# Group statistics on TensorE, the layer-2 residual on VectorE, and a new order of the third stage, in a four-layer convolution kernel

## The chip, the cores and the metric

The kernel runs on one core of a Trainium2 chip. The metric is the device time of one execution, in microseconds, taken as the median of several runs. Unless marked ns, all times below are microseconds.

## The reference

The input x is an image batch of shape (8192, 8, 16, 16): 8192 samples, 8 channels, 16 rows, 16 columns. Four layers follow, each of the form "normalize, transform, add to the input":

```python
x = x + L0(gn(x))     # a tensor-train operator over (8, 16, 16), plus bias
x = x + L1(gn(x))     # 3x3 convolution, batch norm over the whole batch, relu
x = x + L2(gn(x))     # 3x3 convolution on numbers rounded to int8 range, scale from max|gn(x)|
x = x + L3(gn(x))     # 3x3 convolution with weights sign(w) * mean|w|, edge padding

def gn(v, G=4, eps=1e-5):          # per sample and group of two channels: 512 numbers
    m, s = mean(g), var(g)         # over 2 channels, 16 rows, 16 columns
    return (g - m) / sqrt(s + eps)
```

Two sums go over everything and so cut the kernel into stages: the batch norm of layer 1 needs statistics of all samples, and the scale of layer 2 needs the largest absolute value of all normalized samples.

## The kernel before

**Tiling.** The batch is cut into NT = 64 tiles of 128 samples. A tile is held as [128 partitions, 2048]: the partition is (channel, row), 128 in all, and along the free axis stand 128 samples of 16 columns each. One tile is 1 MB. A group of the normalization is 32 partitions times the 16 numbers of a sample, so its sums need an addition across partitions and one across the 16 columns, and its results have to be spread back over the 32 partitions.

**Stages.** Stage 1 (to about 2640) computes layer 0 and the convolution of layer 1, and writes x and y of most tiles to memory. Stage 2 (lines 746 to 865; about 2640 to 3063) loads them, applies batch norm and relu (`sum2`), takes the group statistics, subtracts the mean (`centre2`), finds the largest normalized value (`range2`), and stores the centred tile, except for 13 tiles that stay on the chip. Stage 3 (lines 880 to 1053; 3063 to the end) rounds and convolves for layer 2, adds, takes new group statistics, convolves for layer 3, adds, and stores.

**Group statistics before.** `sums_pe` (line 708) multiplies the tile, and then its square, by `wsum`, a [128, 32] matrix that adds each group's 32 partitions. It is called on four quarters of 512 columns, each of which fills 32 rows of PSUM (32 samples of 16 columns), so that the four quarters stand in the four column groups of the TensorE array:

```python
for k, src in ((0, x), (1, sq)):
    for q in range(NQ):
        pe.matmul(ps[32 * q:32 * q + 32], L["wsum"][:, k], src[:, q * BANK:(q + 1) * BANK], ...)
```

VectorE then adds over the 16 columns (`tensor_reduce` in `stats_small`, line 719, and `stats2`, line 781) and transposes blocks of 32 by 32, so that samples stand on partitions and the four groups along the free axis; variance and `pow` (on GpSimd, line 729) follow on [128, 4]. To come back, `to_rows` (line 732) writes the four numbers of each sample through a mask into a [128, 4, 32] block diagonal, transposes that on VectorE, and TensorE multiplies the result by a selection matrix (`sel0`, `sel1`, `corr`), which gives a [128 partitions, 128 samples] array in PSUM. VectorE reads that array with each value repeated over the 16 columns (`over_w`).

**The steps of stage 3, for one tile.** The names are those of the dictionary `OPS` (line 1032) and are used in what follows:

- `rows2`, `spread2`: 1/sigma of stage 2, times the scale, spread over partitions (PSUM `ps_a`).
- `v` (line 925, VectorE): x times that, written as int8. `q` (933, ScalarE): v as bf16.
- `c2h0`, `c2h1` (942, TensorE): layer 2, six bf16 products for each half of the tile, into PSUM tiles `pq` of a pool `ps_c` with two buffers.
- `bias` (938, ScalarE) and `stz` (951, VectorE): bias and residual of the first half. `z1` (955, ScalarE) and `add1` (958, GpSimd): those of the second half.
- `sq`, `sums` (962, 965): the square on ScalarE and `sums_pe`; `small` (969, VectorE), `pow` (973, GpSimd): the statistics.
- `rows3`, `spread3`: three sets of rows, two products (`ps_r`, `ps_o`).
- `t` (982, VectorE): x/sigma. `hi` (993, ScalarE): t rounded to float32r, and its edge columns copied (`edges`). `lo` (998, GpSimd): t minus hi; `edl` (1011, ScalarE): its edges. Both hi and lo have two buffers (pool `wk3`).
- `c`, `corr` (976, 1003): the part of layer 3 that comes from mean and bias, evaluated on ScalarE and added by GpSimd; for the last three tiles VectorE does it.
- `c3h0`, `c3h1` (1014, TensorE): layer 3, twelve float32r products for each half (six of hi, six of lo), into `pf`, from the same pool as `pq`. `out0`, `out1` (1025, VectorE): scale and residual; the second of them issues the store.

**What sets the order.** All engine calls go through `InOrder` (line 33), which keeps them in the order in which the program makes them. Each engine works its own list from the front; the framework puts in the waits for data and for buffers. So an order written in the program is the order on each engine. In stage 2 that is the loop at lines 852 to 865. In stage 3 it is the list `todo` (line 1044): a turn `TURN`, in which each step stands with an offset in tiles, repeated; its first 151 and last 130 entries are replaced by the lists `C_HEAD` and `C_TAIL`, written out by hand. Loads of stage 3 (`load3`, line 896) are issued on the SP queue with `rows2`, four tiles ahead; x tiles have 13 slots, and the stores to the result stand on the same queue.

In the trace all recorded engine calls have line 43, so groups are told apart by tile names: `pf` (layer 3), `pq` (layer 2), `s` and `gs` (sums in stage 3 and 2), `ps_a`, `ps_r`, `ps_o`, `gb`, `gr` (spreads).

Of the kernel before, what the change touches and what calls it, by code (L numbers as in the profile page):

```python
# [18 lines left out]
P = 128  # L19
# [28 lines left out]
C_HEAD = """  # L48
rows2:0 spread2:0 v:0 rows2:1 q:0 spread2:1 c2h1:0 rows2:2 bias:0 v:1 spread2:2 rows2:3 c2h0:0 v:2 z1:0 q:1
spread2:3 stz:0 add1:0 bias:1 c2h1:1 sq:0 c2h0:1 z1:1 v:3 sums:0 stz:1 small:0 q:2 add1:1 c2h0:2 c2h1:2 bias:2  # L50
rows2:4 pow:0 sq:1 rows2:5 rows3:0 z1:2 spread2:4 spread3:0 stz:2 t:0 q:3 sums:1 hi:0 c:0 small:1 v:4 add1:2 pow:1
bias:3 c2h0:3 spread2:5 rows3:1 sq:2 c2h1:3 spread3:1 stz:3 lo:0 sums:2 t:1 rows2:6 corr:0 edl:0 small:2 c:1 q:4
z1:3 hi:1 c3h0:0 pow:2 c3h1:0 v:5 add1:3 rows3:2 out0:0 bias:4 out1:0 lo:1 sq:3 q:5 spread3:2 spread2:6 c2h0:4 c:2
corr:1 edl:1 c2h1:4 rows2:7 z1:4 stz:4 t:2 hi:2 sums:3 c3h1:1 small:3 v:6 c3h0:1 out1:1 c2h1:5 pow:3 bias:5 rows3:3
spread3:3 lo:2 out0:1 q:6 spread2:7 rows2:8 z1:5 edl:2 v:7 c:3 add1:4 sq:4 c2h0:5 c3h0:2 bias:6 t:3 corr:2 stz:5
sums:4 c3h1:2 small:4 add1:5 hi:3 out0:2 c2h0:6 pow:4 rows3:4 sq:5 out1:2 spread2:8 stz:6 spread3:4 t:4 lo:3 c2h1:6
z1:6 corr:3 edl:3 sums:5 c:4 hi:4 small:5 pow:5 bias:7 v:8 q:7 add1:6
""".split()
C_TAIL = """
c2h1:-4 sq:-5 rows2:-2 rows3:-6 out1:-8 spread3:-6 rows2:-1 spread2:-2 c2h0:-4 v:-2 sums:-5 stz:-4 z1:-4 q:-3 t:-6  # L60
edl:-7 c3h0:-7 q:-2 small:-5 c2h1:-3 c:-6 out0:-7 c2h0:-2 hi:-6 add1:-4 sq:-4 pow:-5 rows3:-5 z1:-3 spread3:-5
bias:-2 t:-5 stz:-2 lo:-6 edl:-6 sums:-4 small:-4 bias:-3 corr:-6 c:-5 spread2:-1 c2h0:-3 stz:-3 pow:-4 c3h1:-7
hi:-5 out1:-7 c3h0:-6 rows3:-4 spread3:-4 add1:-3 c2h1:-2 sq:-3 lo:-5 z1:-2 out0:-6 v:-1 c3h1:-6 edl:-5 q:-1 add1:-2
sums:-3 t:-4 corr:-5 c:-4 c3h1:-5 out1:-6 small:-3 sq:-2 pow:-3 hi:-4 out1:-5 lo:-4 rows3:-3 bias:-1 sums:-2 c2h1:-1
small:-2 z1:-1 spread3:-3 edl:-4 c2h0:-1 c3h0:-5 c:-3 t:-3 stz:-1 add1:-1 pow:-2 corr:-3 rows3:-2 c3h1:-4 hi:-3
spread3:-2 sq:-1 out0:-5 c:-2 corr:-4 sums:-1 t:-2 lo:-3 hi:-2 small:-1 pow:-1 out1:-4 c3h0:-4 corr:-2 rows3:-1
out0:-4 edl:-3 c3h0:-3 spread3:-1 t:-1 lo:-2 c3h1:-3 out0:-3 edl:-2 out1:-3 hi:-1 c:-1 lo:-1 c3h0:-2 c3h1:-2 edl:-1
out0:-2 c3h0:-1 out1:-2 corr:-1 c3h1:-1 out0:-1 out1:-1
""".split()

# [8 lines left out]
def tile_net(ctx: ExitStack, tc: tile.TileContext, xb, xt_in, pack0, pack1, pack2, out):  # L79
# [84 lines left out]
    def late_constants(late):  # L164
# [99 lines left out]
        mod32 = const.tile([P, 32], F32, name="mod32")  # L264
# [5 lines left out]
        for k, name in enumerate(("sel0", "sel1", "corr")):  # L270

            t = L[name] = const.tile([P, CH], F32, name=name)
            dve.tensor_copy(t.rearrange("p (g n) -> p g n", g=G),
                            mod32[:, G * k:G * k + G].unsqueeze(2).to_broadcast([P, G, CH // G]))
        yield "statistics"

    def diagonal(n):
        ts = []
        for k in range(2):
            t = const.tile([P, NQ, 32], F32, name=f"diag_{n}_{k}")  # L280
            nc.gpsimd.memset(t, 0.0)
            ts.append(t)
        return ts
# [424 lines left out]
    def sums_pe(ps, x, sq):  # L708

        for k, src in ((0, x), (1, sq)):  # L710
            for q in range(NQ):
                pe.matmul(ps[32 * q:32 * q + 32], L["wsum"][:, k], src[:, q * BANK:(q + 1) * BANK],
                          start=(k == 0), stop=(k == 1))


    def put_quarter(ps):
        nc.vector.tensor_copy(ps[:, 0:NQ], L["quarter"])

    def stats_small(mv, st, ps, name):

        s = small.tile([P, 32], F32, name=f"s_{name}", tag="s")
        dve.tensor_reduce(s, samples(ps), AX.X, ALU.add)
        dve.transpose(st, s)
        sq = small.tile([P, G], F32, name=f"sq_{name}", tag="sqm")
        dve.tensor_copy(mv[:, 0:G], st[:, 0:G])
        dve.tensor_tensor(sq, st[:, 0:G], mv[:, 0:G], ALU.mult)
        dve.scalar_tensor_tensor(mv[:, G:2 * G], st[:, G:2 * G], EPS, sq, ALU.add, ALU.subtract)

    def stats_pow(mv):
        pool.tensor_tensor(mv[:, G:2 * G], mv[:, G:2 * G], mhalf[:, :G], ALU.pow)  # L730

    def to_rows(diag, mask, cols, name):

        at = 0
        for c in cols:
            n = c.shape[1]
            dve.tensor_tensor(diag[:, :, at:at + n], c.unsqueeze(1).to_broadcast([P, NQ, n]),
                              mask.unsqueeze(2).to_broadcast([P, NQ, n]), ALU.mult)
            at += n
        rows = small.tile([P, P], F32, name=f"rows_{name}", tag="rows")  # L740
        dve.transpose(rows, diag.rearrange("p q j -> p (q j)"))
        return rows

# [5 lines left out]
    with tc.tile_pool(name="p2", bufs=2) as p2, tc.tile_pool(name="ps2", bufs=2, space=PSUM) as ps2:  # L749
# [3 lines left out]
        diag = diagonal("b")  # L753
        psc, mask2 = (ps2.tile([P, 96], F32, name=n, tag=n, bufs=1) for n in ("psc2", "mask2"))
        put_quarter(mask2)
        mask2 = mask2[:, 0:NQ]

# [7 lines left out]
        nc.vector.tensor_tensor(L["corr"], L["corr"], ksum, ALU.subtract)  # L765

# [10 lines left out]
        def sums2(i):  # L777
            T[i]["ps"] = ps2.tile([P, BANK], F32, name=f"gs_{i}", tag="gs")
            sums_pe(T[i]["ps"], T[i]["x"], T[i].pop("sq"))

        def stats2(i):

            st, mv = psc[:, 32 + 32 * (i % 2):64 + 32 * (i % 2)], gnst[:, order2[i]]
            red = small.tile([P, 32], F32, name=f"s_c{i}", tag="s")
            dve.tensor_reduce(red, samples(T[i].pop("ps")), AX.X, ALU.add)
            dve.transpose(st, red)
            T[i]["sq"] = small.tile([P, G], F32, name=f"sq_c{i}", tag="sqm")
            act.copy(mv[:, 0:G], st[:, 0:G])
            act.activation(T[i]["sq"], st[:, 0:G], AF.Square)

        def sigma2(i):
            st, mv = psc[:, 32 + 32 * (i % 2):64 + 32 * (i % 2)], gnst[:, order2[i]]
            dve.scalar_tensor_tensor(mv[:, G:2 * G], st[:, G:2 * G], EPS, T[i].pop("sq"), ALU.add, ALU.subtract)
            stats_pow(mv)

        def spread2(i):
            T[i]["gb"] = ps = ps2.tile([P, BANK], F32, name=f"gb_{i}", tag="gb")
            rows = to_rows(diag[i % 2], mask2, [gnst[:, order2[i]]], f"c{i}")
# [5 lines left out]
            for dst, sel in ((ps[:, 0:P], L["sel0"]), (T[i]["gr"][:, i % 4], L["sel1"])):  # L804
                pe.matmul(dst, sel, rows, start=True, stop=True)

        def centre2(i):
            x, ps = T[i]["x"], T[i]["gb"]
            engines = [dve, dve]
            if NT - 4 <= i < NT - 1:  # L810
                engines, mean = [dve, pool], small.tile([P, P], F32, name=f"gm_{i}", tag="rows")
# [33 lines left out]
        for i in range(NT + 4):  # L845
# [9 lines left out]
            on(i - 2, sums2)  # L855
            on(i - 3, spread2)
            on(i - 1, square2)
# [22 lines left out]
    with ExitStack() as s:  # L880
        wk = s.enter_context(tc.tile_pool(name="wk3", bufs=2))
# [7 lines left out]
        diag2, diag3 = diagonal("d"), diagonal("e")  # L889

        ps_a, ps_r, ps_o = (ps_s.tile([P, BANK], F32, name=f"ps_{n}", tag=n) for n in ("a", "r", "o"))
        r2, r3, o3 = ps_a[:, 0:P], ps_r[:, 0:P], ps_o[:, 0:P]
        put_quarter(ps_a[:, P:2 * P])
        mask, st3 = ps_a[:, P:P + NQ], ps_a[:, P + 32:P + 64]

# [11 lines left out]
        def rows2(i):  # L907
            T[i]["rows2"] = to_rows(diag2[i % 2], mask, [gnst[:, order[i], G:2 * G]], f"d{i}")

        def rows3(i):  # L910
            mv = T[i].pop("mv")
            mr = small.tile([P, G], F32, name=f"mr_{i}", tag="mr")
            dve.tensor_tensor(mr, st3[:, 0:G], mv[:, G:2 * G], ALU.mult)
            T[i]["rows3"] = to_rows(diag3[i % 2], mask, [mr, mv[:, G:2 * G], gnst[:, order[i], 0:G]], f"e{i}")


        def spread2(i):
            pe.matmul(r2, L["sel0"], T[i].pop("rows2"), start=True, stop=True)

        def spread3(i):  # L920
            rows = T[i].pop("rows3")
            pe.matmul(r3, L["sel1"], rows, start=True, stop=True)
            pe.matmul(o3, L["corr"], rows, start=True, stop=True)
# [14 lines left out]
        def bias2(i):  # L938
            x = halves(T[i]["x"])[:, 0]
            act.activation(x, x, AF.Identity, bias=L["bias2"], scale=1.0)  # L940

# [9 lines left out]
        def first2(i):  # L951
            x = halves(T[i]["x"])[:, 0]
            dve.scalar_tensor_tensor(x, T[i].pop(("pq", 0)), inv, x, ALU.mult, ALU.add)

        def second2(i):
            act.activation(z3[i % 2], T[i].pop(("pq", 1)), AF.Identity, bias=L["bias2"], scale=inv)

        def add2(i):
# [3 lines left out]
        def square3(i):  # L962
            act.activation(sq3, T[i]["x"], AF.Square)
# [159 lines left out]
```

## Time and profile before

| what | value |
|---|---|
| median of 3 runs | 3832.61 (3832.19 to 3832.81) |
| span of the profiled execution | 3831.5 |
| PE busy | 3606.5 (94%), 16326 instructions |
| DVE busy | 3406.9 (89%), 6319 |
| ACT busy | 2513.1 (66%), 2673 |
| POOL busy | 3040.9 (79%), 3101 |
| DMA | 960.93 MB, mean 251 GB/s |
| span 2640 to 3063 (stage 2): PE, DVE, ACT, POOL busy | 248.7, 392.4, 247.8, 347.4 of 422.9; DMA share 0.94 |
| span 3063 to 3831 (stage 3): PE, DVE, ACT, POOL busy | 747.0, 697.0, 577.0, 711.0 of 768.6; DMA share 0.41 |

PE is TensorE, PEld its weight loads, DVE VectorE, ACT ScalarE, POOL GpSimd, SP the engine whose queue issues most DMAs. A line of the timeline gives start, duration, engine, operation, output and inputs with shapes, and the number of instructions merged; in brackets stands the time for which the engine was idle before it, and what ended that. Durations of pipelined instructions overlap, so the distance from one start to the next is not the duration. A float32 product leaves two records in the trace, a float32r or bf16 product one.

### The profile page before, as it was taken

How to read it: one execution, taken by the hardware profiler on the slowest of the kernel's cores; microseconds unless marked ns; L12 is line 12 of the kernel's file. 1: busy time of each engine (PE TensorE's matmuls, PEld its weight loads, DVE VectorE, ACT ScalarE, POOL GpSimd, SP SyncE). 2: the span in 40 equal slices, each digit the busy share in tenths (PEclk: the TensorE clock that was granted, in tenths of full speed). 3: DMA queues.
4: the chain of work that ended last, by engine and by line, in shares of the span. 5: the costliest groups of instructions: out<-in, count | busy, mean ns of one | idle time of the engine just before them, and what ended most of it. 6: DMA issues, size and time to landing. Idle time of an engine off the chain costs nothing. (4 is left out here: it accounts for less than half of the span.)

```text
span 3831.5 us, 52833 instructions
## 1 busy us (share of the span) xinstructions
PE 3606.5 (94%) x16326; PEld 2127.6 (56%) x16326; DVE 3406.9 (89%) x6319; ACT 2513.1 (66%) x2673; POOL 3040.9 (79%) x3101
## 2 busy tenths in 40 slices
PE   8999999999999999999999999997655599999998
PEld 4666666666666666666666666662211155555555
DVE  8988888888888888888888888877998889999997
ACT  5666666666666666666666666665665477777775
POOL 4877778777777787777777877766887779999997
PEclk9999999999999999999999999998776699999999
DMA  5787787888877878788788788757999724444432
GB/s 212 255 268 258 258 266 251 270 253 262 270 256 258 267 250 271 253 262 267 258 261 266 250 271 252 258 187 281 422 425 425 301 110 176 187 185 178 185 145 99
DMA packets 210809, 960.93 MB, mean 251 GB/s; under 512 B 44896, under 2 KB 45152, under 8 KB 110048
## 3 DMA queue, kind: packets, MB, share of 16 engines
q1 hardware_dynamic: 173808, 692.22, 48.7%
q0 software_dynamic: 36288, 264.26, 23.4%
q8 instruction: 131, 2.15, 0.2%
q14 instruction: 150, 1.23, 0.1%
q10 hardware_dynamic: 432, 1.08, 0.1%
HBM read 578.84 MB, written 378.54 MB: 250 GB/s over the span
## 5 line engine op out<-in xcount | busy, mean ns | idle before, releaser
L43 PE MATMUL po<-u,core 128*128 128x512 f32 (+1 forms) x4112 | 1844.7, 591 | 0.0
L43 ACT COPY u<-pu 128x2048 f32<-128x2048 f32 x512 | 956.7, 1868 | 511.9 <-PE pu L43 511.8
L43 PEld LDWEIGHTS po<-u,core 128*128 128x128 f32 x4112 | 744.7, 190 | 737.1 <-issue 736.1
L43 PE MATMUL pu<-core2r,xl 128*128 128x256 f32 x4032 | 678.5, 310 | 4.5 <-ACT u L43 3.6
L43 PEld LDWEIGHTS pu<-core2r,xl 128*128 128x128 f32 x4032 | 527.9, 189 | 127.8 <-issue 123.0
L43 POOL TENSOR_TENSOR bs<-bs,xh 128x512 fp32r<-128x512 f32 (+1 forms) x253 | 325.6, 1287 | 201.0 <-ACT xh L43 200.9
L43 POOL TENSOR_TENSOR v<-e 128x128 f32<-128x128 f32 x750 | 397.9, 542 | 0.0
L43 DVE TENSOR_TENSOR xs<-po,xs 128x512 f32<-128x512 f32 x256 | 177.0, 692 | 217.5 <-PE po L43 217.5
L43 ACT ACTIVATE m<-pm,b 128x128 f32<-128x128 f32 x250 | 92.0, 368 | 395.5 <-PE pm L43 395.5
L43 PEld LDWEIGHTS pm<-v,fast 128*128 128x128 f32 x2000 | 262.5, 191 | 119.7 <-issue 106.2
L43 POOL TENSOR_TENSOR e<-x1n,x 128x512 f32<-128x512 f32 x250 | 306.2, 1225 | 23.9 <-ACT x L43 16.4
L43 DVE TENSOR_TENSOR bs<-bs,stat 128x1024 f32<-128x1024 f32 x252 | 290.8, 1217 | 2.1
L43 POOL TENSOR_TENSOR xs<-xs,w 128x2048 f32<-128x2048 f32 x64 | 291.5, 4554 | 0.6 <-DMA xs<-in_xt 0.6
L43 PE MATMUL pm<-v,fast 128*128 128x128 f32 x2000 | 263.6, 275 | 0.0
L43 ACT ACTIVATE x<-x1n 128x512 f32<-128x512 f32 x500 | 247.1, 545 | 7.6 <-DVE x1n L43 7.6
L43 POOL TENSOR_TENSOR mv<-mv,mhalf 128x4 f32<-128x4 f32 x127 | 130.8, 1030 | 138.1 <-DVE mv L43 138.1
L43 PE MATMUL pf<-hi,sign 128*128 128x512 f32 x768 | 227.7, 434 | 0.5 <-DVE xs L43 0.5
L43 POOL DMA_DIRECT2D xl<-limb_d x252 | 150.0, 595 | 96.9 <-ACT x L43 29.1
L43 PE MATMUL pf<-lo,sign 128*128 128x512 f32 x768 | 219.4, 423 | 0.0
L43 POOL TENSOR_TENSOR v<-r 128x128 f32<-128x128 f32 x500 | 215.9, 448 | 0.0
L43 ACT ACTIVATE sq<-xs 128x2048 f32<-128x2048 f32 x103 | 196.8, 1911 | 4.7 <-POOL xs L43 4.6
L43 PE MATMUL gb<-rows_c,sel 128*128 128x128 f32 x128 | 40.3, 409 | 167.3 <-DVE rows_c L43 167.3
(310 smaller groups left out, 7202.4 us busy)
## 6 DMA issues: line engine op xcount, KB each, us to landing
xl<-limb_d POOLq DMA_DIRECT2D x252, 1024.0 KB, 7.4
x_d<-xs SPq DMA_DIRECT2D x76, 1024.0 KB, 8.4
xs<-in_xt SPq DMA_DIRECT2D x64, 1024.0 KB, 7.5
bs<-in_xb SPq DMA_DIRECT2D x63, 1024.0 KB, 5.7
limb_d<-xh SPq DMA_DIRECT2D x1008, 64.0 KB, 4.3
limb_d<-bs SPq DMA_DIRECT2D x1008, 64.0 KB, 5.2
y_d<-ys SPq DMA_DIRECT2D x60, 1024.0 KB, 8.0
u<-x_d SPq DMA_DIRECT2D x34, 1024.0 KB, 5.9
```

Of the source, the lines that this page charges most:

```text
L43: return self.tc.keep_in_program_order(op(*args, **kwargs))
```

## The change

1. **Sums.** `sums_pe` no longer gives one product to a quarter of 512 columns, but one to each of the 16 image columns w: 128 samples, 16 elements apart in memory, added up in PSUM over w. Four column groups take w modulo 4. The result is [4 x 32, 128 samples], where before it was [4 x 32, 512].
2. **Transposes.** ScalarE copies that result to SBUF (`S`), and one product with it as the weights against eight columns of `mod32` (`fold`) adds the four column groups and puts samples on partitions. To come back in stage 2 and in `spread2` of stage 3, ScalarE widens each sample's numbers to 32 equal columns (`wide`) and a product with the identity transposes them. In stage 3 the three sets of rows stand in one [128, 128] tile `rows3[k]`; a product with the identity turns it (`rT`), ScalarE copies it (`rows`), and `r3` and `o3` spread it as before. Square of the mean is on ScalarE (`sq4`), variance and ratio on VectorE (`var`, `mr`).
3. **Layer 2's residual** is `stz0` and `stz1`, both on VectorE without bias. The bias goes into the square (`sq`), into the copied sums (`sbias`), into `t` (now a three-operand instruction) and into `c` (`bias23`). `bias`, `z1` and `add1` are gone.
4. **Order of stage 3.** `TURN`, `C_HEAD` and `C_TAIL` are replaced by a phase for each step and a period; step `op` of tile i stands at 10.78 i + phase. The special case of the last three tiles in `c` and `corr` is gone, the edges of hi are a step of their own (`edh`), and the second half of layer 3 stands ahead of the first. PSUM of stage 3 has a further bank (`ps_t`).

```diff
+PERIOD = 10.78
+PHASE = {"wide": 0, "spread2": 0.01, "v": 0.02, "q": 11, "c2h0": 13.3, "stz0": 18.2, "c2h1": 19.6, "stz1": 21.4, "sq": 25.8,
+         "sums": 31.9, "S": 33.2, "fold": 36.4, "sq4": 36.8, "var": 41.5, "pow": 48.2, "mr": 51.2, "m2": 53.8, "rT": 55.5,
+         "rows": 56.7, "r3": 59.8, "t": 61.9, "hi": 65.3, "o3": 67.3, "c": 68.6, "edh": 69.1, "lo": 73.4, "corr": 75.7,
+         "edl": 76.6, "c3h1": 84.2, "out1": 85.4, "c3h0": 86.3, "out0": 86.31}
...
     def sums_pe(ps, x, sq):
         for k, src in ((0, x), (1, sq)):
-            for q in range(NQ):
-                pe.matmul(ps[32 * q:32 * q + 32], L["wsum"][:, k], src[:, q * BANK:(q + 1) * BANK],
-                          start=(k == 0), stop=(k == 1))
+            for w in range(W):
+                rows = slice(32 * (w % 4), 32 * (w % 4) + 32)
+                pe.matmul(ps[rows], L["wsum"][:, k], samples(src)[:, :, w], start=(k == 0 and w < 4), stop=(k == 1 and w >= W - 4))
+    def fold_pe(st, rows):
+        pe.matmul(st, rows, L["mod32"][:, 0:2 * G], start=True, stop=True)
+    def wide(dst, src):
+        act.copy(dst.rearrange("p (g n) -> p g n", n=CH // G), src.unsqueeze(2).to_broadcast([P, src.shape[1], CH // G]))
+    def spread_pe(dst, col):
+        pe.matmul(dst, col, ident, start=True, stop=True)
...
             on(i - 2, sums2)
+            on(i - 3, wide2)
+            on(i - 2, copy2)
             on(i - 3, spread2)
+            on(i - 2, fold2)
...
-        def second2(i):
-            act.activation(z3[i % 2], T[i].pop(("pq", 1)), AF.Identity, bias=L["bias2"], scale=inv)
-        def add2(i):
-            x = halves(T[i]["x"])[:, 1]
-            pool.tensor_tensor(x, x, z3[i % 2], ALU.add)
+        def first2(i, h):
+            x = halves(T[i]["x"])[:, h]
+            dve.scalar_tensor_tensor(x, T[i].pop(("pq", h)), inv, x, ALU.mult, ALU.add)
...
         def square3(i):
-            act.activation(sq3, T[i]["x"], AF.Square)
+            act.activation(sq3, T[i]["x"], AF.Square, bias=L["bias2"], scale=1.0)
+        def copy3(i):
+            T[i]["S"] = small3.tile([P, P], F32, name=f"S_d{i}", tag="S", bufs=2)
+            act.activation(T[i]["S"], s3[i % 2], AF.Identity, bias=L["sbias"], scale=1.0)
+        def fold3(i):
+            fold_pe(st3[i % 2], T[i].pop("S"))
+        def sigma3(i):
+            dve.scalar_tensor_tensor(rows3[i % 2][:, G:2 * G], st3[i % 2][:, G:2 * G], EPS, T[i].pop("sqm"), ALU.add, ALU.subtract)
+        def ratio3(i):
+            dve.tensor_tensor(rows3[i % 2][:, 0:G], st3[i % 2][:, 0:G], rows3[i % 2][:, G:2 * G], ALU.mult)
+        def turn3(i):
+            pe.matmul(turned, rows3[i % 2], ident, start=True, stop=True)
+        def rows_copy3(i):
+            T[i]["rows"] = small3.tile([P, P], F32, name=f"rows_{i}", tag="rows")
+            act.copy(T[i]["rows"], turned)
...
         def scale3(i):
-                dve.tensor_tensor(samples(t)[:, a:b], samples(x)[:, a:b], over_w(r3, a, b), ALU.mult)
+                dve.scalar_tensor_tensor(samples(t)[:, a:b], samples(x)[:, a:b], L["bias2"], over_w(r3, a, b), ALU.add, ALU.mult)
         def high3(i):
             act.copy(hi[:, :, 1:W + 1], samples(T[i]["t"]))
-            edges(hi)
...
-        todo = [(op, i + k) for i in range(-3, NT + 4) for op, k in TURN if 0 <= i + k < NT]
-            todo = head + todo[len(head):len(todo) - len(tail)] + tail
+        todo = [(op, i) for _, op, i in sorted((PERIOD * i + at, op, i) for op, at in PHASE.items() for i in range(NT))]
         for op, i in todo:
-            if op == "rows2" and AHEAD <= i + 4 < NT:
+            if op == "spread2" and AHEAD <= i + 4 < NT:
                 load3(i + 4)
             OPS[op](i)
```

In this order one turn reads as follows, with tile k at the end of its way, engine by engine:

- TensorE: spread2(k+8), c3h0(k), rT(k+3), c2h0(k+7), o3(k+2), fold(k+5), r3(k+3), c3h1(k+1), c2h1(k+7), sums(k+6).
- VectorE: v(k+8), out0(k), stz0(k+7), t(k+3), mr(k+4), var(k+5), out1(k+1), stz1(k+7).
- ScalarE: wide(k+8), q(k+7), hi(k+2), S(k+5), edl(k+1), rows(k+3), c(k+2), sq(k+6), edh(k+2), sq4(k+5), m2(k+4).
- GpSimd: corr(k+1), pow(k+4), lo(k+2).

## The prediction

> **What bounds the kernel now.** I read the slices of the page first, then one period of stage 3 in the timeline, engine by engine, then stage 2 by stretches.
>
> ```profile
> PE   8999999999999999999999999997655599999998
> DVE  8988888888888888888888888877998889999997
> POOL 4877778777777787777777877766887779999997
> DMA  5787787888877878788788788757999724444432
> ```
>
> Each digit is the busy share of a slice of 95.8 us. Stage 2 (2640 to 3063 us) has DMA at 9s and PE at 5 to 7; stage 3 (3063 to 3831) has PE, DVE and POOL all at 9. A share can't rank those three, so I take one tile of stage 3, as TensorE ran it:
>
> ```profile
> 3399.91 1.71 PE L43 MATMUL pf<-lo,sign 128*128 128x512 f32 x6
> 3401.46 1.72 PE L43 MATMUL pf<-hi,sign 128*128 128x512 f32 x6
> 3403.02 1.71 PE L43 MATMUL pf<-lo,sign 128*128 128x512 f32 x6
> 3404.57 1.47 PE L43 MATMUL pq<-q,band 128*128 128x512 bf16 x6
> 3405.88 0.39 PE L43 MATMUL ps_a<-rows_d,sel 128*128 128x128 f32 x2
> 3406.10 0.39 PE L43 MATMUL ps_r<-rows_e,sel 128*128 128x128 f32 x2
> 3406.32 0.39 PE L43 MATMUL ps_o<-rows_e,corr 128*128 128x128 f32 x2
> 3406.55 1.46 PE L43 MATMUL pq<-q,band 128*128 128x512 bf16 x6
> 3407.94 1.06 PE L43 MATMUL s<-ys,wsum 128*32 128x512 f32 x8
> 3408.82 1.04 PE L43 MATMUL s<-sq,wsum 128*32 128x512 f32 x8
> 3409.79 1.82 PE L43 MATMUL pf<-hi,sign 128*128 128x512 f32 x6
> ```
>
> The durations overlap; start to start is what an operation costs. Six pf take 1.555, six pq 1.31, a 128-column product 0.22 (two records), the sums 1.85. The next pf starts at 3411.45, so the period is 11.54, with no gap. The least sum is 6.22 (24 pf) + 2.62 (12 pq) + 0.66 + 1.75 = 11.25. GpSimd does nearly as much:
>
> ```profile
> 3396.95 3.69 POOL L43 TENSOR_TENSOR u<-u,c 128x2048 f32<-128x2048 f32 x1
> 3400.61 2.42 POOL L43 TENSOR_TENSOR ys<-ys,bs 128x1024 f32<-128x1024 f32 x1
> 3402.98 1.02 POOL L43 TENSOR_TENSOR mv<-mv,mhalf 128x4 f32<-128x4 f32 x1
> 3404.28 4.27 POOL L43 TENSOR_TENSOR lo<-xh,hi 128x2048 fp32r<-128x2048 f32 x1 [0.28 <-POOL mv L43]
> ```
>
> That is 11.40 of 11.55. So both bind: relieving GpSimd alone leaves TensorE's 11.25, at most 0.3 per tile, and TensorE has no room for more work. VectorE's same period has two waits of 0.23 in it, so some 11.1 of work.
>
> Stage 2 by stretches of 20 us:
>
> ```profile
> 2840.00:2860.00 20.00, 10.60 (x60) 3.79 (x56) 19.43 (x30) 12.83 (x13) 17.38 (x7) 0.75 1.01 425
> 2960.00:2980.00 20.00, 11.15 (x56) 3.63 (x52) 15.62 (x25) 10.92 (x10) 14.15 (x7) 0.65 1.01 424
> ```
>
> DMA is full from 2660 to 3020. VectorE (the third pair: 19.43, then 15.62) is full too at first, as it eats up the tiles loaded ahead, but later it waits for loads, one tile in 7.4 us. Only after the last DMA wait (2997) does VectorE alone set the pace.
>
> [...] 16 f32 records of the sums, each 0.427 on the full array (po: 8 in 3.42), cost 1.75, a quarter. [...] at 46.95 us four 32-row records start every 0.21, 53 ns each[...]
>
> ```profile
> L43 DVE TENSOR_REDUCE mod<-ident x1: 374/374/374, 87.2 to 87.2; 128x32 f32<-128x128 f32 x1
> L43 DVE TENSOR_REDUCE grp<-ident x1: 275/275/275, 34.8 to 34.8; 128x4 f32<-128x128 f32 x1
> ```
>
> Both reduce 128 elements, mod with a stride of 128 bytes; less a one-element copy (0.145) that is 1.8 against 1.0 ns each. No row has TensorE reading so.
>
> **The change, part by part.**
>
> *Stage 2.* VectorE loses the reduce (0.65), a transpose (0.23), diag (0.18) and a transpose (0.31), some 1.4 of 6.07; ScalarE gains two small copies (about 0.3 each), TensorE the fold. While DMA is full this is worth nothing. After 2997 tiles go by 5.6 (GpSimd's 4.55 + 1.02) instead of 6.07: about 2.4 over the last six. From the last add (3036.6) to the maximum (3063) before takes 26.3, in rounds of 5.3; the new chain for the last tiles (pow 1.02, wide 0.3, product 0.5, centre 2.3, range 2.3, each handed on) is some 20. Gain 8.5; bounds 0 (if the sums grow) and 15. ScalarE's wide copy now stands behind the relu that waits for a load; centring stands behind that, but needs only about 7.7 from the relu's start and overlaps the next tile, so a 7.4 us period hides it. The SP order of loads and stores is unchanged.
>
> *Stage 3, TensorE.* Three small products become four (+0.22) and a fold, 128x128 weights against 8 columns. No row shows that; the nearest has the same weights and 128 columns (0.22), and [...] I take 0.25; bounds 0.1 and 0.4. Sums: the same 4096 columns, but 32 products of 128 columns with a moving stride of 64 bytes. No row has that stride on TensorE. Bounds: 1.75 (columns alone decide; fewer columns would be needed for a gain) and 7.1 [...]. Between lies half rate, 3.5. I take 1.75 to 1.8, since the total of columns is what the 1.75 was spent on, and keep the others as rivals. Least per tile: 6.22 + 2.62 + 0.88 + 0.25 + 1.75 = 11.7.
>
> *GpSimd and VectorE.* GpSimd loses the add (2.42): 8.98. VectorE loses reduce, transposes, diag and copies (about 2.6), gains a second residual (1.2), and t becomes three-operand (2.38 for two). About 10.2. ScalarE loses bias (1.15) and z1 (1.21), gains wide, S, rows: about 8.5. All fit under 11.7: nothing gained, since TensorE doesn't shrink.
>
> *The new order, a new wait.* This is the part that decides. Read one turn of the new order with tile k: TensorE has c3h0(k), turn, c2h0, o3, fold, r3, c3h1(k+1), c2h1, sums, spread. ScalarE has hi(k+2), S, edl(k+1), rows, in this order. hi (the rounded half of t) has two buffers, so hi(k+2) can't be written until c3h0(k), the last reader of hi(k), is done; in the old order both halves of tile k were through a turn earlier. The built program shows it: hi waits for VectorE alone before, for VectorE and TensorE after. Queued behind it is rows, which TensorE needs for its r3 product, which stands before c3h1(k+1). From the end of c3h0's last slot: the rest of that record 0.17 (0.43 long, slots of 0.26), handing over 0.04 (pq ends 3408.01, ScalarE starts 3408.05), hi 1.83 (start to start, as the square before c), S 0.27 and rows 0.35 (c is 0.34), edl 0.43, to TensorE 0.15 (rows_c ends 2851.33, gb starts 2851.48): 3.24. Meanwhile TensorE has the turn (0.22), six pq (1.31), o3 (0.22), fold (0.25): 2.0. It idles 1.24 each tile. Period: spread 0.22 + c3h0 3.11 + 3.24 + r3 0.22 + c3h1 3.11 + pq 1.31 + sums 1.8 = 13.0, +1.46. Bounds of the idle: 0 and 1.6.
>
> *Start and end.* Hand-tuned beginning and end fall away. Before, the first pf starts 33 after 3064. In the new order ScalarE alone has 7 q, 5 squares, 2 hi and some 25 small copies (32 us) before edl of tile 0; followed by hand in order, with the waits between engines (some 14 us, most while VectorE makes the first v and residuals), c3h1 starts about 46 after (40 to 52). Then 57 periods of 13.0 (741), then six shrinking ones (12.7, 11.4, 9.6, 9.6, 9.4, 7, the last paced by hi, lo, edl: 60), the last twelve and twelve pf 6.2, result and store 6.4. Sum 860; before 3831.5 - 3064.5 = 767: +93. SP: loads are asked for four tiles ahead as before; the store that frees their slot is issued a period earlier and lands in about 8.4, under 11.5, so no load waits long in front of the stores behind it. GpSimd's queue holds no DMA here.
>
> Sum: 3831.5 + 93 - 8.5 = 3916 as span; the median of the runs (3832.6) stands 1.1 above the span, so 3917.
>
> **The rivals.**
>
> *Strided reads at half rate.* Sums 3.5, period 14.7: +1.7 on 59 tiles is +100: 4017. For: the two reductions above. Against: an f32 record already spends 0.83 ns a column (0.427 for 512)[...]. Slower still (7.1): 4230.
>
> *The chain doesn't bite.* Period 11.75: (0.2 x 60) + 13 + 4 - 8.5 = +20 at most, 3840 to 3853.
>
> *TensorE's 100% is elastic; GpSimd sets the pace* (the page warns that ends are modelled). Then the period falls to VectorE's 10.2 plus some waiting, 10.7: -0.85 x 60 - 8.5 = -60: 3773. It decides if TensorE's work with the added 0.45 takes under 11.5 and no chain binds. Against: at the very end, with nothing else running, 48 pf take 12.7, 0.26 each, as in the middle.
>
> **How the numbers follow.** Likeliest case (own range 3885 to 3955) 0.46; half rate (3970 to 4048) 0.31; slower reads 0.08; no chain 0.06; GpSimd's pace 0.09. From 3838 to 4050 leaves out 0.08 + 0.09 and some 0.03 of edges. Within 0.2% (7.7 us, about what a measurement here can tell) ends mostly a part of the no-chain case: 0.03; faster 0.09; slower 0.88.
>
> **What would show it.** Stage 3's period, c3h0 to c3h0: 13.0 with a TensorE idle of 1.2 before r3, released by ScalarE's rows; hi waiting for TensorE on ScalarE; GpSimd at about 70%. The sums, start to start: 1.8 or 3.5. Stage 2's maximum near 3054. First pf some 46 after it. It is wrong if the period is under 11.6, if rows never keeps TensorE waiting, or if the sums cost over 2.2.

## The result, and the profile after

| | before | after |
|---|---|---|
| median of the runs (range) | 3832.7 (3832.2 to 3833.7) | 4042.9 (4042.1 to 4043.7) |
| span of the profiled execution | 3831.5 | 4040.2 |
| last maximum of stage 2 starts | 3062.3 | 3062.2 |
| first `pf` of stage 3 | 3097.9 | 3119.0 |
| one tile of stage 3, mean between 3200 and 3700 | 11.55 | 14.98 |

The changed kernel is slower: ratio 1.0549, with a 95% interval of 1.0534 to 1.0564, so +210. The forecast was 3917. Its direction held, and the time is inside its range, but the mechanism that I held likeliest is not what made most of the difference.

The slices of the page of the changed kernel, each now 101 us:

```profile
PE   8999999999999999999999999977667999999998
DVE  8988888888888888888888888777677666666665
POOL 4877777777777787777777777498784655565556
DMA  6877888878787888787878787499991333333322
```

In the last nine slices, all of stage 3, VectorE fell from 9 to 6 and GpSimd from 9 to 5 or 6; only TensorE is still at 9. So the change did relieve both engines, and the bill of stage 3 is on TensorE. One turn of stage 3 in TensorE's timeline of the changed kernel (start, duration, out<-in, records; in brackets idle time before it and what ended it):

```profile
3517.09 0.49 PE L43 MATMUL ps_a<-ident,wide_d 128*128 128x128 f32 x2
...
3518.97 1.73 PE L43 MATMUL pf<-lo,sign 128*128 128x512 f32 x6
3521.50 0.46 PE L43 MATMUL ps_t<-ident,rows 128*128 128x128 f32 x2 [0.80 <-ACT S_d L43]
...
3523.31 0.29 PE L43 MATMUL ps_a<-mod,S_d 128*128 128x8 f32 x2
3523.45 0.47 PE L43 MATMUL ps_r<-rows,sel 128*128 128x128 f32 x2
...
3528.28 2.06 PE L43 MATMUL ps_t<-xs,wsum 128*32 128x128 f32 x32
3530.15 2.07 PE L43 MATMUL ps_t<-sq,wsum 128*32 128x128 f32 x32
3532.15 0.49 PE L43 MATMUL ps_a<-ident,wide_d 128*128 128x128 f32 x2
```

From 3517.09 to 3532.15 is the period. The sums, start to start, take 3532.15 - 3528.28 = 3.87; before they took 1.85. This is one of the longer turns: periods of 15.04, 15.05, 14.91, 14.95 and 14.98 follow each other over and over, and the sums in them go from 3.72 to 3.87. The means are 14.98 and 3.80, and these are used below; the expectations took 15.04 and 3.87 from one turn. What makes this pattern was not tried.

There is an idle of 0.80, but ahead of the turn product (`ps_t<-ident,rows`), not ahead of r3 (`ps_r`), which waits for nothing. Over the mean period, +3.43 are 1.95 of sums and 1.48 of the rest. ScalarE's side of the same place, one turn earlier:

```profile
3504.13 1.93 ACT L43 CAST hi<-xh 128x2048 fp32r<-128x2048 f32 x1 [5.79 <-PE pf L43]
3505.96 0.36 ACT L43 ACTIVATE S_d<-ps_t,sbias 128x128 f32<-128x128 f32 x1
```

`hi` waits 5.79 for TensorE; that it would wait for TensorE was foreseen. S stands behind it; and the turn product waits for S. Why it should wait for S, whose data it doesn't use, is the second question of the experiments.

### The profile page after: what moved, and what is told of

It reads as the page before. It is cut to its first block, busy times and chain, and to the rows that moved or that the text cites. A ratio compares the mean times of both kernels' runs of the same rounds, so it can differ in the third digit from the quotient of the medians.

```text
span 4040.2 us, 65740 instructions
## 1 busy us (share of the span) xinstructions
PE 3817.9 (94%) x22856; PEld 2392.7 (59%) x22856; DVE 3272.5 (81%) x5481; ACT 2462.9 (61%) x2996; POOL 2905.3 (72%) x3036
## 5 line engine op out<-in xcount | busy, mean ns | idle before, releaser
L43 POOL TENSOR_TENSOR lo<-sq,hi 128x2048 fp32r<-128x2048 f32 x32 | 137.1, 4285 | 180.4 <-ACT hi L43 174.2
L43 POOL TENSOR_TENSOR lo<-xh,hi 128x2048 fp32r<-128x2048 f32 x32 | 137.1, 4284 | 175.8 <-ACT hi L43 175.8
L43 PE MATMUL pq<-q,band 128*128 128x480 bf16 (+1 forms) x768 | 189.2, 383 | 1.1 <-ACT q L43 1.1
```

The source lines that it names most:

```text
L43: return self.tc.keep_in_program_order(op(*args, **kwargs))
```

## The experiments

Theory A: the sums doubled because their moving operand is read with a step of 64 bytes. Rival B: because they are 64 short records instead of 16 long ones. Theory C: the idle comes from the turn product and the sums lying in one PSUM bank. Rival D: from the chain hi, S, edl, rows wherever it is waited for.

**a_contig**: as many products, of neighbouring columns.

```diff
-  pe.matmul(ps[rows], L["wsum"][:, k], samples(src)[:, :, w], ...)
+  pe.matmul(ps[rows], L["wsum"][:, k], src[:, w * P:(w + 1) * P], ...)
```

> The changed kernel with one edit: product w of the sums reads 128 neighbouring columns instead of every 16th, in stages 2 and 3, so the statistics are of the wrong elements (that part of the computation is changed); number, shape and order of the products stay. Theory A (the 64-byte step of the moving operand costs): the sums fall from 3.87 to about 1.85 per tile, stage 3's period from 15.04 to about 13.0 with the idle of 0.80 left in place, the time to about 4043 - 57 x 2.02 - 10 = 3918. Rival B (64 short products cost by their number, about 58 ns each): sums 3.7 to 3.9 and 4043 as before. Between: a sum of about 2.8 would mean both. In stage 2, A lets the last maximum come earlier than 3062 only if the sums held it; I expect less than 3 us.

3923.7; ratio to before 1.0235 (1.0218 to 1.0252). Its TensorE timeline:

```profile
3512.43 1.08 PE L43 MATMUL ps_t<-xs,wsum 128*32 128x128 f32 x32
3513.33 1.06 PE L43 MATMUL ps_t<-sq,wsum 128*32 128x128 f32 x32
3514.31 0.49 PE L43 MATMUL ps_a<-ident,wide_d 128*128 128x128 f32 x2
...
3518.71 0.46 PE L43 MATMUL ps_t<-ident,rows 128*128 128x128 f32 x2 [0.80 <-ACT S_d L43]
```

64 records in 1.88 (29 ns each), against 16 records in 1.85 before: their number costs nothing here. B falls, A stands. The idle is untouched, the period is 13.07. So 119 of the 210 are the step alone: 14.98 - 13.07 = 1.91 in each turn, which is what the sums lost.

**b_step16**: the other way round, the kernel before with its long products, but a step of 64 bytes in them.

```diff
-  src[:, q * BANK:(q + 1) * BANK]
+  src.rearrange("p (b w) -> p w b", w=W)[:, 4 * q:4 * q + 4]
```

> The kernel before with one edit: its 16 records of 512 columns for the sums read four samples' columns interleaved, 16 elements (64 bytes) apart, in stages 2 and 3 (the reduction after them then adds other elements: statistics changed). Number and shape of products stay those of before. Theory A: sums 1.85 to about 3.9, period 11.54 to 13.55, time about 3833 + 60 x 2.0 = 3953. Rival B (number of products): sums 1.85, 3833.

3931.6; ratio 1.0257 (1.0242 to 1.0273). Its timeline:

```profile
3506.47 1.90 PE L43 MATMUL s<-xs,wsum 128*32 128x512 f32 x8
3508.18 1.91 PE L43 MATMUL s<-sq,wsum 128*32 128x512 f32 x8
3510.02 1.80 PE L43 MATMUL pf<-hi,sign 128*128 128x512 f32 x6
```

The sums take 3.55, the period 13.15: +98, where I expected +120. So the step by itself nearly doubles the old sums too, from 1.85 to 3.55. The 0.25 a tile that is missing to the mean of 3.80 appears only where the step and the short records come together; why was not tried.

**a_step2, a_step3, a_step4**: the products of a_contig with a step of 8, 12 and 16 bytes.

```diff
+  src[:, w // 2 * 256 + w % 2:(w // 2 + 1) * 256:2]                 # a_step2
+  src[:, w // 4 * 512 + w % 4:w // 4 * 512 + w % 4 + 382:3]         # a_step3
+  src[:, w // 4 * 512 + w % 4:(w // 4 + 1) * 512:4]                 # a_step4
```

> As the contiguous variant, but each product reads every 2nd column (8 bytes apart) out of 256 (statistics of the wrong elements). Under A, if the cost goes by the 16-byte pieces that a product touches (32 when contiguous, 64 here, 128 at a step of 64 bytes): 1.85 + 2.02 x (64 - 32) / (128 - 32) = 2.5 for the sums, period 13.7. If only steps over some width cost: 1.85. If any step costs the whole price: 3.87. B: 3.87.

> As before, with every 4th column (16 bytes apart) out of 512 (statistics of the wrong elements). By 16-byte pieces the cost is that of the 64-byte step: sums 3.87, period 15.0. If it is by 32-byte or 64-byte pieces, it lies between: about 2.9 or 2.3. B: 3.87 too, which is why the contiguous variant goes beside it.

> The changed kernel with every product of the sums reading every 3rd column (12 bytes apart; statistics of the wrong elements). Steps of 8 bytes cost as contiguous reads (sums 1.95), steps of 16 as those of 64 (3.8). Theory A1 ([...] the cost follows the pieces touched): 96 pieces for 128 columns, three quarters of a step of 16: 3.87 x 0.75 = 2.9, period 14.1, time about 3985. Rival A2 (a step of at most 8 bytes is read two at a time, anything wider one by one): 3.87, 4043.

| step, bytes | 16-byte pieces per column | sums, mean | time |
|---|---|---|---|
| 4 (a_contig) | 1/4 | 1.88 | 3923.7 |
| 8 (a_step2, one run) | 1/2 | 1.96 | 3928.5 |
| 12 (a_step3, one run) | 3/4 | 2.91 | 3987.8 |
| 16 (a_step4, one run) | 1 | 3.78 | 4042.9 |
| 64 (after) | 1 | 3.80 | 4042.9 |

Of my readings for a_step2, that only steps over some width cost came out (1.96, not 2.5). a_step3 then told two of them apart, and the one by pieces gave 2.9 and 3985 beforehand. Its timeline:

```profile
3516.54 1.59 PE L43 MATMUL ps_t<-xs,wsum 128*32 128x128 f32 x32
...
3519.45 0.49 PE L43 MATMUL ps_a<-ident,wide_d 128*128 128x128 f32 x2
```

All five rows are near 3.8 times the pieces per column, but never under about 1.9: with two columns to a piece (a_step2) the sums still take 1.96, against 1.88 with four, and with one they take 3.78 (a_step4) and 3.80 (after), about twice that. Why a piece with one column costs so much was not shown.

**a_turn**: the turned rows in another PSUM bank.

```diff
-  r2, r3, o3, turned = (t[:, 0:P] for t in (ps_a, ps_r, ps_o, ps_t))
+  r2, r3, o3, turned = ps_a[:, 0:P], ps_r[:, 0:P], ps_o[:, 0:P], ps_r[:, P:2 * P]
```

> The changed kernel with the turned rows put beside r3 in its PSUM bank instead of beside the sums of stage 3. Theory C (the turn product waits for the copy S only because S reads the same bank): the idle of 0.80 before the turn goes, and as rows would then be ready some 0.4 before r3 is due, no idle takes its place: period 15.04 - 0.80 = 14.24, time 4043 - 0.80 x 58 = 3997. Rival D (the chain hi, S, edl, rows on ScalarE binds wherever it is waited for): the idle moves to just before r3, released by rows, 0.4 to 0.8 of it, period 14.6 to 15.0, time 4018 to 4043.

3984.7; ratio 1.0397 (1.0381 to 1.0412). Its timeline, TensorE and then ScalarE:

```profile
3509.31 1.73 PE L43 MATMUL pf<-lo,sign 128*128 128x512 f32 x6
3510.87 0.39 PE L43 MATMUL ps_r<-ident,rows 128*128 128x128 f32 x2
```

```profile
3509.51 1.93 ACT L43 CAST hi<-xh 128x2048 fp32r<-128x2048 f32 x1 [5.72 <-PE pf L43]
3511.34 0.35 ACT L43 ACTIVATE S_d<-ps_t,sbias 128x128 f32<-128x128 f32 x1
```

`hi` still waits, S is still late (3511.34), but the turn product starts ahead of it, and no other idle takes its place. D falls: the wait was not for data, and putting the rows elsewhere removes it, as C said. In this kernel each of these PSUM tiles fills one whole bank (the kernel's `BANK`, 512 numbers on each partition), so no run tells a wait for the bank from one for the tile that fills it. Here the turned rows and the sums were different columns of `ps_t`; who put this wait in, no run shows. The period fell to 13.95 in the mean, by 1.03 and not by 0.80: the product before an idle also runs out alone (pf<-lo to the turn product 1.56 here, 1.73 + 0.80 there), and the turn product itself takes 0.22 instead of 0.29. Together these are 0.97 + 0.07: the idle cost more here than its bracket says.

**a_hi3**: three buffers for `hi`; the bf16 `q` moves to space that stage 3 no longer uses.

```diff
-  q = wk.tile([P, F], BF16, name=f"q_{i}", tag="q")
+  q = z3[i % 2].bitcast(BF16)
-  ... name=f"hi_{i}", tag="hi")
+  ... name=f"hi_{i}", tag="hi", bufs=3)
```

> The changed kernel with three buffers for hi instead of two (the bf16 q lies in space that stage 3 no longer uses, so that they fit). If hi's wait for TensorE is the root of the chain: ScalarE's wait before hi (5.8 per tile) goes or moves to VectorE, S is done before the turn product wants it, the idle of 0.80 goes, period 14.24, time about 3997. If S is late for another reason than hi (the sums themselves end late), the idle stays, 4043.

3981.5 in one run; period 13.95, no idle, and `hi` has no wait for TensorE among its waits. So either remedy suffices: S was late because of the two buffers, and lateness of S mattered because of what it shares with the turned rows.

**a_contig_turn**: both edits in one.

> Both edits in one: contiguous (wrong) columns for the sums and the turned rows beside r3 (statistics of the wrong elements). If the two costs add: period 13.91 - 2.0 = 11.9, time 3985 - 2.0 x 59 = 3867. If the chain through ScalarE bites once TensorE's turn is shorter: an idle before r3 of 0.4 to 1.2 and 3890 to 3930.

3860.0 in one run; sums 1.89, period 12.03. The two costs add, within 7 us of the expectation. In the two turns from 3501.48 to 3525.53 TensorE's timeline has no wait.

**a_old3**: stage 3's sums as before the change, with the reduction and the 32x32 transpose on VectorE; the rest of the change stays (turned rows as in a_turn).

```diff
-  sums_pe(s3[i % 2], T[i]["x"], sq3)
+  for k, src in ((0, T[i]["x"]), (1, sq3)):
+      for q in range(NQ):
+          pe.matmul(ps_t[32 * q:32 * q + 32], L["wsum"][:, k], src[:, q * BANK:(q + 1) * BANK], ...)
-  act.activation(T[i]["S"], s3[i % 2], AF.Identity, bias=L["sbias"], scale=1.0)
+  dve.tensor_reduce(T[i]["red"], samples(ps_t), AX.X, ALU.add)
+  act.activation(T[i]["S"], T[i].pop("red"), AF.Identity, bias=sbias16, scale=1.0)
-  fold_pe(st3[i % 2], T[i].pop("S"))
+  dve.transpose(st3[i % 2], T[i].pop("S"))
```

> The changed kernel with the sums of stage 3 alone as they were before the change: 16 records of 512 neighbouring columns, VectorE's reduction and 32x32 transpose instead of S at 128 columns and the fold; turned rows beside r3 as in the variant with the turn moved. New order, turn product, residual on VectorE stay. Expected: period 15.04 - 0.80 (idle) - 2.02 (sums) - 0.14 (fold) = 12.08, time about 4043 - 2.96 x 58 = 3871: so still slower than before by about 0.5 a tile, which is the added small product and the restarts of the pf groups. If VectorE (some 10.2 of work in the changed kernel, 11.1 with these two operations) binds instead, waits of TensorE for VectorE appear and the period is over 12.3.

3936.5 (ratio 1.0271, 1.0254 to 1.0289), a miss by 65. TensorE's r3, then two operations of VectorE in the same turn:

```profile
3511.38 0.49 PE L43 MATMUL ps_r<-rows,sel 128*128 128x128 f32 x2 [1.17 <-ACT rows L43]
```

```profile
3508.51 1.28 DVE L43 SCALAR_TENSOR_TENSOR ys<-pf,scale,ys 128x1024 f32<-128x1024 f32 x1 [0.74 <-PE pf L43]
3509.71 0.68 DVE L43 TENSOR_REDUCE red_d<-ps_t 128x32 f32<-128x512 f32 x1
```

The sums are 1.85 again, but TensorE idles 1.17 before r3: I had put the reduction behind the residual of the `pf` half, so it starts 4.8 after the sums are done (3504.9), and S and rows follow. This is an idle where the prediction had one, before r3 and for rows, but made by a queue on VectorE.

**a_old3b**: the reduction ahead of `v` in VectorE's queue, S ahead of `hi` in ScalarE's.

```diff
-  "sums": 31.9, "S": 33.2,
+  "sums": 31.9, "red": 31.95, "S": 32.4,
```

> The variant with the old sums in stage 3, with VectorE's reduction ahead of v instead of behind the second result in its queue, and S ahead of hi on ScalarE. If the idle of 1.17 before r3 is this stand in the queue: it goes, period 13.16 - 1.17 = 12.0, time 3936 - 1.17 x 58 = 3869. If rows stays late because hi waits for the pf products: idle 0.4 to 1.2 stays, 3890 to 3936.

3874.5 (ratio 1.0108, 1.0093 to 1.0123); period 12.12, and r3 still starts 0.3 late, for rows. It was the place in the queues, for all but that; the two moves were not tried apart.

**a_pair**: the change's sums, but each product takes two neighbouring w of every sample, 8 bytes out of 64; turned rows as in a_turn.

```diff
-  for w in range(W):
-      pe.matmul(ps[rows], L["wsum"][:, k], samples(src)[:, :, w], ...)
+  for j in range(W // 2):
+      pe.matmul(ps[rows].rearrange("p (b t) -> p b t", t=2), L["wsum"][:, k], samples(src)[:, :, 2 * j:2 * j + 2], ...)
-  pe.matmul(st, rows, L["mod32"][:, 0:2 * G], start=True, stop=True)
+  for t in range(2):
+      pe.matmul(st, rows[:, t * P:(t + 1) * P], L["mod32"][:, 0:2 * G], start=(t == 0), stop=(t == 1))
```

> The changed kernel with the turned rows beside r3, and the sums as 16 products of 256 columns that read two neighbouring w of each of the 128 samples (8 bytes out of every 64) instead of 32 products of 128 columns that read one; the fold then adds the two with a second product, S is copied at 256 columns. It computes what the changed kernel computes. Under A1 (pieces touched): half as many pieces per column as with the 64-byte step, so the full rate, sums 3.87 to about 1.9, period 13.91 - 1.97 + 0.14 = 12.1, time 3985 - 1.83 x 58 = 3879. Under A2 (any gap over 8 bytes anywhere in the access costs): 3.6 to 3.9 and about 3990.

3874.2 (ratio 1.0107, 1.0091 to 1.0124). Its timeline:

```profile
3520.08 1.10 PE L43 MATMUL ps_t<-u,wsum 128*32 128x256 f32 x16
3521.00 1.07 PE L43 MATMUL ps_t<-sq,wsum 128*32 128x256 f32 x16
3522.00 0.49 PE L43 MATMUL ps_a<-ident,wide_d 128*128 128x128 f32 x2
```

Sums 1.92: two columns to a piece bring back the full rate, though the pieces still lie 64 bytes apart. This is the theory's strongest test, since it keeps the wide gaps and computes what the changed kernel computes. With the turn moved it takes 169 off the changed kernel. The period is 12.29, 0.2 over my estimate: the second fold product costs 0.22 where I took 0.14, and the sums, 3.80 in the mean and not 3.87, had less to lose.

**b_resid**: of the change only the residual, all on VectorE, put into the kernel before.

```diff
-  x = halves(T[i]["x"])[:, 0]                              # bias, ScalarE: now the whole tile
+  x = T[i]["x"]
-  act.activation(z3[i % 2], T[i].pop(("pq", 1)), AF.Identity, bias=L["bias2"], scale=inv)
-  pool.tensor_tensor(x, x, z3[i % 2], ALU.add)
+  dve.scalar_tensor_tensor(x, T[i].pop(("pq", 1)), inv, x, ALU.mult, ALU.add)
```

> The kernel before with one part of the change alone: layer 2's residual of both halves on VectorE straight from PSUM (the bias put on the whole tile by ScalarE beforehand), GpSimd's addition of 2.42 and ScalarE's z copy taken out; order, sums and transposes as before. If relieving GpSimd is what counts: period 11.54 to 11.25 at best, 3833 - 0.29 x 58 = 3816. If VectorE then binds: 11.1 + 1.2 = 12.3, +0.76 x 58 = +44, 3877, with TensorE waiting for VectorE.

3941.8 (ratio 1.0284, 1.0269 to 1.0300); period 12.91. GpSimd has 31% free now (345 of 500 us), and 109 are lost: VectorE binds. My 12.3 was too little because of my own edit, as its timeline shows:

```profile
3503.21 2.48 DVE L43 SCALAR_TENSOR_TENSOR xs<-pq,inv,xs 128x1024 f32<-128x1024 f32 x2 [0.92 <-ACT xs L43]
```

VectorE's period is 12.0 of work and this wait for a bias that now takes ScalarE 2.0 instead of 1.15. So moving GpSimd's addition to VectorE does not pay by itself, but the size for the change's own form of it (bias folded into later steps) isn't measured by this run.

No variant beats the kernel before.

## Why the prediction was right and wrong

*What bounds.* Right: TensorE is full (496 of 500 us before, between 3300 and 3800), and relief elsewhere bought nothing; in a_contig_turn, with both costs out, its own work still makes the period of 12.03. GpSimd was forecast at 8.98 a tile and VectorE at some 10.2; in the same stretch of the changed kernel they are busy 300 and 334 of 500 us, that is 9.0 and 10.0 of 14.98.

*The sums: the step that failed.* "I take 1.75 to 1.8, since the total of columns is what the 1.75 was spent on." They take 3.80: this term of the period, put at 1.8, is 2.0 too small, and that is most of the error. a_contig and b_step16 show that the step of 64 bytes does it, at +1.92 and +1.70. The rival "at half rate" had 3.5, and its 4017 was nearer than my 3917; its period of 14.7 against 14.98 is some 16 of the 26 that it lacked. My ground against it, the 0.83 ns that an f32 record already spends on a column, was a guess about slack that no row showed. And I let VectorE's two reductions (1.8 against 1.0 ns an element) count for little: reckoned over four column groups, b_step16's 8192 column reads in 3.55 are 1.73 ns each, close to that price; whether the cause is the same was not tried. My bound of 7.1 was an estimate that had the price twice for each of these reads; no run showed that.

*The idle: size near, cause and place wrong.* I had 1.24 before r3. It is 0.80 (1.03 with its surroundings, by a_turn), before the turn product. Two errors offset each other, which is luck. First, I let `hi` wait for the end of `c3h0`; but the six products of hi stand first in it, and `hi` starts at 3504.13, when they end (3504.09), one lot of six (1.57) earlier. From there the 3.24 of ScalarE stand against 1.57 + 2.0 = 3.57 of TensorE, and r3 doesn't wait at all. Second, I missed that the turned rows share a PSUM tile with what S reads; that wait has only the 1.57 of the lo products to cover it. a_contig, which has sums as I forecast them, came to a period of 13.07 against my 13.0 and 3923.7 against 3917. That agreement is partly luck. In the steady turns both signs of being wrong that the prediction names for these two steps are there: sums over 2.2, and rows that never keep TensorE waiting.

*The small products.* Foreseen +0.47 (0.22 and 0.25). In a_turn, with no idle, the period is 13.95: +2.40 over before, of which 1.95 are sums, so 0.45 for the small products and all else. The fold costs 0.14 itself, in the low part of my bounds.

*Stage 2: gain of 8.5, measured 0.* Groups of VectorE by form, changed kernel:

```profile
L43 DVE TENSOR_REDUCE amax<-top x16: 685/686/687, 2665.4 to 3062.2; 128x1 f32<-128x512 f32 x16
```

The last maximum stands where it stood. The 2.4 from a shorter period came: the last eight adds are 39.5 apart, from 2997.95 to 3037.44, against 41.9 before. But they begin 3.3 later, because the loads before them land 3.3 later; the DMA was full in both kernels (share 1.01 between 2960 and 3000), and why they land later was not tried. And from the last add to the maximum is 24.8, not 20 (before: 25.7), because ScalarE's `wide` waits for `pow`, which on GpSimd stands behind an add and a centring:

```profile
3044.99 0.40 ACT L43 COPY wide_c<-gnst 128x256 f32<-128x256 f32 x1 [4.84 <-POOL gnst L43]
```

The sum closes: +3.3 - 2.4 - 0.9 = 0. My chain had pow in it, but not its place in GpSimd's queue. It isn't the strided sums: in a_contig, without the step, the maximum starts at 3063.0, no earlier.

*Start and end.* The first `pf` comes 54.6 after 3064.4, when VectorE has scaled stage 2's 1/sigma; forecast were 46. In a_contig_turn, with both costs out, it comes 45.9 after the same point, as forecast: the early tiles pay the same two bills. The sum from the kernel before: first `pf` 21 later, 57 periods of 3.43 more (196), 8 less at the end (what is left over), together 209 of span.

## What to carry to other kernels

Before a product's operand is rearranged, count how many of its columns each 16-byte piece of SBUF serves: with two (a_pair, a_step2) the sums by short, gapped fp32 products here took 1.92 and 1.96, near the 1.88 without gaps, and with one (after, a_step4) 3.80 and 3.78. When an instruction waits for another whose data it doesn't use, look for what else lies in the PSUM tile that both touch, here one whole bank, and move that first: it was worth 1.03 a tile in a_turn. And when work is moved off two engines onto the one that is already full, price the moved work on that engine first: here GpSimd and VectorE came down to 9.0 and 10.0 of busy time a tile, and the tile went from 11.55 to 14.98.

## What was not expected of the hardware

64 records of 128 columns cost as much as 16 of 512 (1.88 and 1.85), 29 ns a record start to start with four column groups in turn. With a step of 64 bytes the short ones do cost more (3.80 against 3.55), and only there do the sums vary from turn to turn, by 0.15 in a pattern of five; in a_contig they stay within 0.01. A step of 12 bytes costs in between (2.91, three quarters of the 3.78 at 16 bytes give 2.84), so here the price follows the pieces touched and is no switch. A product against 8 columns with 128x128 weights takes 0.14, two thirds of one against 128 columns (0.22).
